# Two gather groups of x instead of six, and one-hot rows made by GpSimd in a graph-network kernel

## The chip, the cores and the metric

The kernel runs on one core of a Trainium2 chip. The metric is device time in microseconds of one execution. A core has a matrix engine (TensorE, PE in the profile; its weight loads are PEld), VectorE (DVE), ScalarE (ACT), GpSimd (POOL) and SyncE (SP), which here only issues transfers. Each engine works through its own queue in order; semaphores tie the queues together. SBUF is the on-chip memory of 128 partitions, PSUM the small memory that TensorE writes to.

## What is computed

x has 6250 nodes of 256 values; 100000 edges (src, dst) come sorted by dst. Cut to what matters:

```python
theta_x = (x[dst] - x[src]) @ theta_w.T + theta_b
phi_x = x[src] @ phi_w.T + phi_b
e = relu(theta_x + phi_x)
out = segment_max(e, dst, num_segments=6250)      # 0 where a node has no edge
y = layernorm(x + out)
```

Since the dst part of an edge is the same for all edges of a node, the kernel needs only b = x @ (phi_w - theta_w).T for every node, the maximum of b[src] over each node's edges, and then relu(maximum + x @ theta_w.T + biases) + x, normalised.

## The kernel before

**Two sets of nodes.** Part 1 is nodes 0 to 1129, part 2 the 5120 nodes after (40 tiles of 128, a tile row being one node). Part 1's edges (some 18,700, 146 steps of 128) are all gathered. For part 2 most edges are not gathered: see "parts" below.

**The front** (lines 704 to 784). The rows b of all nodes are made in 13 shares of up to four tiles: load `x_q`, transpose on PE, copy by ScalarE (`x_t`), multiply with the weights (`ps_b`, line 759), copy out and write to `b_rows` in DRAM. `b_of` does this for a pair of tiles. Beside it, GpSimd gathers the first edges of part 1 straight from x, since `b_rows` isn't there yet: `X_GROUPS` groups of `STEPS` = 8 gathers (one gather is 128 rows of 1 KB, one indirect DMA). Their b is then computed per edge (`x_group`, four pairs by `b_of`), which costs PE work but no wait. Two pauses (short iotas, `paced`) follow each of these gathers.

**Runs.** `run` (line 679) is the running maximum along the steps of a group on VectorE (line 688, one instruction per step of 128 x 256), followed by a write of the group to `maxima_1` or `maxima_2` through SP. The gathered groups live in a ring of six buffers (`RING`), tile name `g`.

**The table and the lists.** VectorE sorts the edges of part 2 into a table (`fill_table`), and per slot of 383 source nodes `choice` picks at most one edge of each destination node (nine calls, two slots each); the rest is packed into lists by `list_pieces`, 232 steps long per partition.

**Parts.** For each of 17 slots and each of 5 chunks of 1024 nodes (85 parts, `slot_part`, line 1056), the chosen b rows are fetched by TensorE: a one-hot matrix `hot` (three blocks of 128 x 1024, the last slot one block) times the slot's rows in `terms`, which are split into two terms of lower precision (`slot_terms`, line 1039). A part is 24 matmuls (line 1075); the result goes into the maximum `acc` by VectorE (line 1086; for slot 0 a copy by ScalarE). One block of `hot` takes VectorE one instruction (line 1065) or ScalarE two (lines 1067 and 1068). Which blocks VectorE makes is `dve_hots`: none until `chunk_heads`, then block 0. The second term is a subtraction on VectorE (line 1054). `want`, the row numbers of a part, comes by a transfer through SP. `hot`, `want` and `terms` have two buffers, `raw` one; a part's first matmul reads block 0.

**GpSimd's order is written out**: `in_turn` (line 506) puts each of its operations behind the one before. With list groups the order is: group of 8 gathers, next group of 8 gathers, and so on. `next_group_1` (line 1385) issues the next group of part 1's gathers, the run of the group before, one `node_place` and n parts. It is called nine times between choices, three times within `list_pieces`, once after; then, as long as groups are left, with two parts each. The three gathers of the list's own rows (`dst_w`) stand between the eleventh and the twelfth of these groups. Then follow the 30 list groups (`gather_2`, from b_rows by `list_src`), with the remaining parts spread among them.

**The end** (lines 1273 to 1374, 1447 to 1453). Shares of up to 8 tiles: gather the list maxima, take the maximum with `acc`, add x @ theta_w.T, relu, add x (`rows_of`), then mean, squares and normalise (`normalise`: squares at line 1328 and the normalising at 1338, both on ScalarE, per tile), and write.

The instructions of one engine are placed by a scheduler at build time, by program order and its own estimate of when inputs are ready; only `in_turn` and `behind_in_order` fix more.

Of the kernel before, what the change touches and what calls it, by code (L numbers as in the profile page):

```python
# [58 lines left out]
X_GROUPS = 6  # L59
# [7 lines left out]
DVE_HOTS = 1  # L67
# [3 lines left out]
X_AFTER = 6  # L71
# [356 lines left out]
def gnn_kernel(ctx: ExitStack, tc: tile.TileContext, x, src, dst, theta_w, theta_b, phi_w, phi_b, out):  # L428
# [71 lines left out]
    paced = [2]  # L500
# [209 lines left out]
    with (  # L710
# [59 lines left out]
        for k, share in enumerate(shares(4)):  # L770
# [266 lines left out]
    dve_hots = [0]  # L1037

    def slot_terms(s):
# [3 lines left out]
        rest = left % P  # L1043
        if whole:
            nc.sync.dma_start(raw[:, :whole, :], flat(b_rows, first * D, [[D, P], [P * D, whole], [1, D]]))
        if left < SLOT_ROWS:
            nc.sync.dma_start(raw[rest : rest + 1, whole, :], maxima_2[0:1, :])
        even = rest // 16 * 16
        for a, b in ((0, even), (even, rest)):
            if b > a:  # L1050
                nc.sync.dma_start(raw[a:b, whole, :], flat(b_rows, (first + whole * P + a) * D, [[D, b - a], [1, D]]))
        terms = terms_of[s] = slots.tile([P, PARTS, KB, D], FR, name="terms")
        nc.scalar.copy(terms[:, 0, :n], raw[:, :n])
        nc.vector.tensor_tensor(terms[:, 1, :n], raw[:, :n], terms[:, 0, :n].bitcast(FP), op=ALU.subtract)

    def slot_part(s, c):
# [54 lines left out]
    def list_chunks(ps):  # L1111
# [4 lines left out]
        chunk_0 = work.tile([P, 1], FP, name="chunk_0")  # L1116
# [21 lines left out]
    def list_places():  # L1138

        has = work.tile([P, TILES], FP, name="has")  # L1140
        nc.vector.tensor_tensor(has, up_to[:, 1:], up_to[:, :TILES], op=ALU.is_gt)
        place_f = work.tile([P, TILES], FP, name="place_f")
        nc.vector.tensor_scalar(place_f, up_to[:, 1:], before, -1.0, op0=ALU.add, op1=ALU.add)
        chunk_of = work.tile([P, TILES], FP, name="chunk_of")
# [5 lines left out]
        step = work.tile([P, TILES], I32, name="step")  # L1150
        group = work.tile([P, TILES], I32, name="group")
# [3 lines left out]
        apart = work.tile([P, TILES], FP, name="apart")  # L1155
# [11 lines left out]
    def list_pieces():  # L1167
# [38 lines left out]
        owner = work.tile([P, 1], I32, name="owner")  # L1206
# [31 lines left out]
    def list_carry():  # L1238

        nodes = wide[:, : BACK + LIST_CHUNK]  # L1240
        same = work.tile([P, BACK], FP, name="same_node")
        n_same = work.tile([P, 3], FP, name="n_same")
# [3 lines left out]
        step = work.tile([P, 1], I32, name="carry_step")  # L1246
        group = work.tile([P, 1], I32, name="carry_group")
# [5 lines left out]
        chunk_1 = work.tile([P, 1], FP, name="chunk_1")  # L1253
# [19 lines left out]
    def rows_of(part, j0, n, ps_tile):  # L1273
# [11 lines left out]
        totals = work.tile([P, STEPS], FP, name="totals", bufs=3)  # L1285
# [35 lines left out]
    def normalise(part, j0, n, x_f, totals):  # L1321

        r = work.tile([P, 5, STEPS], FP, name="r")
# [78 lines left out]
    dve_hots[0] = DVE_HOTS  # L1402
# [7 lines left out]
    paced[0] = 1  # L1410
# [8 lines left out]
    paced[0] = 0  # L1419
# [28 lines left out]
    last_shares = [(2, j, STEPS) for j in range(0, TILES - STEPS, STEPS)]  # L1448
    last_shares += [(2, j, STEPS // 2) for j in (TILES - STEPS, TILES - STEPS // 2)]
# [38 lines left out]
```

## Time and profile before

| | |
|---|---|
| median of 3 runs | 747.21 us (745.25 to 751.66) |
| the profiled execution | 743.81 us, its span 741.9 us |
| PE busy | 650.1 us (88%) |
| DVE busy | 640.0 us (86%) |
| POOL busy | 516.5 us (70%) |
| ACT busy | 493.2 us (66%) |
| part matmuls, line 1075 | 1960, 459.7 us busy |
| list gathers (b_rows by list_src) | 232, mean 1008 ns |
| part 1's gathers from b_rows | 98, mean 1342 ns |
| part 1's gathers from x | 48, mean 1267 ns |
| block 0 of `hot` on DVE, line 1065 | 76, mean 760 ns |
| second terms on DVE, line 1054 | 16 of 768 elements, mean 958 ns |
| first gather from b_rows | 111.9 us |
| gathers of the list's own rows | 260.8 us |
| first list gather | 280.2 us |
| last list gather | 610.3 us |
| first gather of part 2's list maxima | 658.9 us |

Busy time is the time in which an instruction of the engine runs; waits and issue gaps between them do not count. Stretches and starts are in microseconds from the span's start. In lists of instructions, "g<-b_rows,list_src" reads: writes tile g, from b_rows by the numbers in list_src; what stands in brackets is the idle time before it and what ended that.

### The profile page before, as it was taken

What the parts mean: (1) busy time and instruction counts of PE and PEld (TensorE: products, weight loads), DVE (VectorE), ACT (ScalarE), POOL (GpSimd) and SP (SyncE); (2) the same over time, 40 slices, a digit from 0 to 9 for tenths busy, and PEclk for the clock granted to TensorE, in tenths of its full rate; (3) what the DMA queues carried; (4) which work ended last, traced back from release to release, by engine and by line L of the source; (5) the groups of instructions that cost most, each with busy time, mean ns of one, the idle gap of its engine ahead of it and who ended that gap; (6) DMA issues with size and microseconds to landing.
All of it is one profiled execution on the core that took longest, in us unless ns stands there. A gap on an engine that the chain in (4) does not pass through costs nothing.

```text
span 741.9 us, 9973 instructions
## 1 busy us (share of the span) xinstructions
PE 650.1 (88%) x3018; PEld 538.2 (73%) x3018; DVE 640.0 (86%) x1197; ACT 493.2 (66%) x700; POOL 516.5 (70%) x561
## 2 busy tenths in 40 slices
PE   1299999839777899999999999999999999789970
PEld 0288888727565788788888888888888888579970
DVE  6699999999996989598979889798878989968881
ACT  0144444459997678687878778777777877037885
POOL 7788987879887787777777777777746373037720
PEclk9999999959998999999999999999999999999995
DMA  6586745585667777988787888778767686535632
GB/s 208 143 282 209 248 157 194 179 285 161 210 206 258 220 251 232 361 267 255 254 261 227 257 242 266 229 258 277 242 223 213 215 255 212 177 107 187 200 142 116
DMA packets 55893, 164.82 MB, mean 222 GB/s; under 512 B 11835, under 2 KB 19796, under 8 KB 48500
## 3 DMA queue, kind: packets, MB, share of 16 engines
q1 hardware_dynamic: 32344, 98.76, 38.5%
q0 software_dynamic: 20944, 57.62, 27.2%
q10 hardware_dynamic: 2540, 7.69, 2.9%
q8 instruction: 27, 0.44, 0.3%
q14 instruction: 38, 0.31, 0.1%
HBM read 101.08 MB, written 63.74 MB: 222 GB/s over the span
## 4 chain that ended last, share of the span: by engine, by line
PE 46%; DVE 14%; ACT 7%; issue 5%; DMA 4%; POOL 2%; DVEq 0%; ACTq 0%; POOLq 0%; SPq 0%
PE ps_f L1075 44%; ACT x_f L1338 3%; DVE acc L1086 3%; ACT squares L1328 3%; DVE g L688 2%; DMA want<-chosen_rows 2%; POOL g L512 2%; PE ps_e L1299 1%; DVE work L1203 1%; DVE hot L1065 1%; DMA g<-b_rows,src 1%; DVE words L1200 1%; DMA dst_w<-list_words,run_start 1%; ACT x_t L1294 1%; DVE x_f L1314 1%
## 5 line engine op out<-in xcount | busy, mean ns | idle before, releaser
L1075 PE MATMUL ps_f<-hot,terms 128*128 128x512 f32 x1960 | 459.7, 396 | 26.2 <-ACT hot L1068 12.2
L1075 PEld LDWEIGHTS ps_f<-hot,terms 128*128 128x128 f32 x1960 | 372.0, 191 | 109.6 <-ACT hot L1068 15.3
L512 POOL DMA_INDIRECT g<-b_rows,list_src x232 | 233.8, 1008 | 92.6 <-issue 63.3
L1067 ACT ACTIVATE hot<-want,minus_row 128x1024 fp32r<-128x1024 f16 x169 | 186.3, 1147 | 95.1 <-PE ps_f L1075 86.3
L1086 DVE TENSOR_TENSOR acc<-acc,ps_f 128x1024 f32<-128x1024 f32 x160 | 193.5, 1216 | 33.2 <-PE ps_f L1075 32.2
L688 DVE SCALAR_TENSOR_TENSOR g<-g,caps 128x256 f32<-128x256 f32 x376 | 180.6, 480 | 9.7 <-DMA g<-b_rows,src 6.7
L1068 ACT ACTIVATE hot<-hot 128x1024 fp32r<-128x1024 f32 x169 | 169.0, 1046 | 0.0
L512 POOL DMA_INDIRECT g<-b_rows,src x98 | 131.5, 1342 | 29.8 <-issue 25.9
L759 PE MATMUL ps_b<-weights,x_t 128*128 128x256 f32 x388 | 89.5, 385 | 1.3 <-ACT x_t L749 0.5
L512 POOL DMA_INDIRECT g<-maxima,place x49 | 47.7, 973 | 52.2 <-DMA maxima<-g 27.2
L759 PEld LDWEIGHTS ps_b<-weights,x_t 128*128 128x128 f32 x388 | 72.1, 191 | 14.3 <-ACT x_t L749 5.0
L512 POOL DMA_INDIRECT g<-in_x_dram,src x48 | 60.8, 1267 | 11.3 <-issue 7.1
L1065 DVE TENSOR_SCALAR hot<-want,row_id 128x1024 fp32r<-128x1024 f16 x76 | 57.6, 760 | 3.0 <-DMA want<-chosen_rows 2.8
L1299 PE MATMUL ps_e<-weights,x_t 128*128 128x256 f32 x192 | 48.4, 380 | 0.2 <-ACT x_t L1294 0.2
L1299 PEld LDWEIGHTS ps_e<-weights,x_t 128*128 128x128 f32 x192 | 32.8, 190 | 3.6 <-ACT x_t L1294 0.5
L762 ACT COPY g<-ps_b 128x512 f32<-128x512 f32 x24 | 14.1, 586 | 29.8 <-PE ps_b L759 28.7
L762 ACT COPY b_sb<-ps_b 128x512 f32<-128x512 f32 (+1 forms) x25 | 14.5, 578 | 28.8 <-PE ps_b L759 24.8
L1294 ACT COPY x_t<-ps_e 128x512 f32<-128x512 f32 x24 | 13.7, 575 | 29.1 <-PE ps_e L1292 29.1
L1338 ACT ACTIVATE x_f<-x_f,r 128x256 f32<-128x256 f32 x49 | 25.3, 590 | 10.0 <-DVE r L1335 10.0
L488 POOL IOTA pause<- 128x160 f32 x102 | 29.2, 287 | 3.3
L749 ACT COPY x_t<-ps_xt 128x512 f32<-128x512 f32 (+1 forms) x49 | 26.1, 593 | 0.0
L1328 ACT ACTIVATE squares<-x_f,r 128x256 bf16<-128x256 f32 x49 | 24.3, 500 | 1.7 <-DVE r L1325 1.7
(266 smaller groups left out, 503.4 us busy)
## 6 DMA issues: line engine op xcount, KB each, us to landing
maxima<-g SPq DMA_DIRECT2D x47, 1024.0 KB
want<-chosen_rows SPq DMA_DIRECT2D x85, 256.0 KB
x_q<-in_x_dram SPq DMA_DIRECT2D x12, 512.0 KB
b_rows<-b_sb ACTq DMA_DIRECT2D x12, 512.0 KB
x_f<-in_x_dram SPq DMA_DIRECT2D x5, 1024.0 KB
out_dram<-x_f SPq DMA_DIRECT2D x5, 1024.0 KB
raw<-b_rows SPq DMA_DIRECT2D x16, 256.0 KB
g<-b_rows,list_src POOLq DMA_INDIRECT x232, 4.6
```

What stands on the lines that cost most here:

```text
L488: return nc.gpsimd.iota(t, pattern=[[step, t.shape[1]]], base=base, channel_multiplier=per_partition, allow_small_or_imprecise_dtypes=True,)
L512: in_turn(nc.gpsimd.indirect_dma_start(out=out, out_offset=out_offset, in_=in_, in_offset=in_offset))
L688: one = nc.vector.scalar_tensor_tensor(g[:, k, :], last[part], caps[:, t : t + 1], g[:, k, :], op0=ALU.min, op1=ALU.max)
L759: nc.tensor.matmul(ps[:, h, :], x_t[:, h, k, :], weights[:, k, 0, :], start=(k == 0), stop=(k == KC - 1))
L1065: nc.vector.tensor_scalar(hot[:, b, :], want, row_id[:, b : b + 1], None, op0=ALU.is_equal)
L1067: nc.scalar.activation(hot[:, b, :], want, AF.Abs, bias=minus_row[:, b : b + 1], scale=1.0)
L1068: nc.scalar.activation(hot[:, b, :], hot[:, b, :].bitcast(FP), AF.Relu, bias=1.0, scale=-1.0)
L1075: nc.tensor.matmul(ps[:, w : w + 512], terms[:, part, b, h * P : (h + 1) * P], hot[:, b, w : w + 512], start=(i == 0), stop=(i == n - 1),)
L1086: latest_part[0] = nc.vector.tensor_tensor(to, to, ps, op=ALU.max).ins.name
L1299: nc.tensor.matmul(a[:, i, :], x_t[:, 2 * i + c, :], weights[:, c, 1, :], start=(c == 0), stop=False)
L1328: nc.scalar.activation(squares, x_f[:, k, :], AF.Square, bias=mean[:, k : k + 1], scale=1.0, accum_out=var[:, k : k + 1])
L1338: nc.scalar.activation(x_f[:, k, :], x_f[:, k, :], AF.Identity, bias=mean[:, k : k + 1], scale=inv[:, k : k + 1])
```

## The change

X_GROUPS goes from 6 to 2, so that four groups of part 1 more are gathered from `b_rows` and need no product of their own. Since 13 calls of `next_group_1` come before the loop over the groups left, four groups then remain for that loop, with two parts each. Block 0 of `hot` is made by GpSimd instead of VectorE, but only from the list groups on; before that ScalarE makes all blocks. The second terms are made by GpSimd throughout. Both operations stand in GpSimd's written order, so they run between groups of gathers. All pauses behind gathers go. The pools of the part tiles are laid out before the front's, the accumulator behind it. At the end the last tiles are cut into shares of 4, 4, 4, 2 and 2, and for the last 16 tiles VectorE does every second normalisation.

```diff
-X_GROUPS = 6
+X_GROUPS = 2
-DVE_HOTS = 1
+POOL_HOTS = 1
-X_AFTER = 6
...
-    paced = [2]
+    paced = [0]
...
-    acc_pool = body.enter_context(tc.tile_pool(name="accs", bufs=1))
-    acc = acc_pool.tile([P, KC, OWN], FP, name="acc")
-
+    work = body.enter_context(tc.tile_pool(name="work", bufs=2))
+    slots = body.enter_context(tc.tile_pool(name="slots", bufs=2))
...
-            nc.sync.dma_start(present(x_q, *share), node_rows(x, *share))
+            x_loaded = nc.sync.dma_start(present(x_q, *share), node_rows(x, *share)).ins.name
...
-            if k == X_AFTER:
-                x_group(of_x[0])
-        for i in of_x[1:]:
+        for i in of_x:
             x_group(i)
 
-    work = body.enter_context(tc.tile_pool(name="work", bufs=2))
-    slots = body.enter_context(tc.tile_pool(name="slots", bufs=2))
+    acc_pool = body.enter_context(tc.tile_pool(name="accs", bufs=1))
+    acc = acc_pool.tile([P, KC, OWN], FP, name="acc")
...
+        for to, rows in pieces:
+            one = nc.sync.dma_start(to, rows)
+            if s == 0:
+                behind_in_order(one, x_loaded, "x ahead of a slot's rows")
         terms = terms_of[s] = slots.tile([P, PARTS, KB, D], FR, name="terms")
         nc.scalar.copy(terms[:, 0, :n], raw[:, :n])
-        nc.vector.tensor_tensor(terms[:, 1, :n], raw[:, :n], terms[:, 0, :n].bitcast(FP), op=ALU.subtract)
+        in_turn(nc.gpsimd.tensor_tensor(terms[:, 1, :n], raw[:, :n], terms[:, 0, :n].bitcast(FP), op=ALU.subtract))
...
-            if b < dve_hots[0]:
-                nc.vector.tensor_scalar(hot[:, b, :], want, row_id[:, b : b + 1], None, op0=ALU.is_equal)
+            if b < pool_hots[0]:
+                in_turn(nc.gpsimd.tensor_scalar(hot[:, b, :], want, row_id[:, b : b + 1], None, op0=ALU.is_equal))
...
-        totals = work.tile([P, STEPS], FP, name="totals", bufs=3)
+        totals = work.tile([P, STEPS], FP, name="totals", bufs=4)
...
-        r = work.tile([P, 5, STEPS], FP, name="r")
+        shared = part == 2 and j0 >= TILES - 2 * STEPS
+        r = work.tile([P, 5, STEPS], FP, name="r", bufs=4)
...
-            nc.scalar.activation(
-                x_f[:, k, :], x_f[:, k, :], AF.Identity, bias=mean[:, k : k + 1], scale=inv[:, k : k + 1]
-            )
+            if shared and k % 2:
+                nc.vector.tensor_scalar(
+                    x_f[:, k, :], x_f[:, k, :], inv[:, k : k + 1], mean[:, k : k + 1], op0=ALU.mult, op1=ALU.add
+                )
+            else:
+                nc.scalar.activation(
+                    x_f[:, k, :], x_f[:, k, :], AF.Identity, bias=mean[:, k : k + 1], scale=inv[:, k : k + 1]
+                )
...
     chunk_heads()
-    dve_hots[0] = DVE_HOTS
...
     list_carry()
-    paced[0] = 1
...
     n_groups = LIST_GROUPS
-    paced[0] = 0
+    pool_hots[0] = POOL_HOTS
...
-    last_shares = [(2, j, STEPS) for j in range(0, TILES - STEPS, STEPS)]
-    last_shares += [(2, j, STEPS // 2) for j in (TILES - STEPS, TILES - STEPS // 2)]
+    widths = [STEPS] * (TILES // STEPS - 2) + [4, 4, 4, 2, 2]
+    assert sum(widths) == TILES
+    last_shares = [(2, sum(widths[:i]), n) for i, n in enumerate(widths)]
```

The rest of the diff gives some fourteen small tiles of the list stage one buffer instead of two, each of them used once.

More of the change, by code (lines that the diff above doesn't have):

```diff
@@ L768, in x_group @@
             run_1(i)
-        for k, share in enumerate(shares(4)):
+        for share in shares(4):
             n = share[2]
@@ L1043, in slot_terms @@
         rest = left % P
+        pieces = []
         if whole:
-            nc.sync.dma_start(raw[:, :whole, :], flat(b_rows, first * D, [[D, P], [P * D, whole], [1, D]]))
+            pieces.append((raw[:, :whole, :], flat(b_rows, first * D, [[D, P], [P * D, whole], [1, D]])))
         if left < SLOT_ROWS:
-            nc.sync.dma_start(raw[rest : rest + 1, whole, :], maxima_2[0:1, :])
+            pieces.append((raw[rest : rest + 1, whole, :], maxima_2[0:1, :]))
         even = rest // 16 * 16
@@ L1149, in list_places @@
         )
-        step = work.tile([P, TILES], I32, name="step")
-        group = work.tile([P, TILES], I32, name="group")
+        step = work.tile([P, TILES], I32, name="step", bufs=1)
+        group = work.tile([P, TILES], I32, name="group", bufs=1)
         nc.vector.tensor_scalar(
@@ L1245, in list_carry @@
         )
-        step = work.tile([P, 1], I32, name="carry_step")
-        group = work.tile([P, 1], I32, name="carry_group")
+        step = work.tile([P, 1], I32, name="carry_step", bufs=1)
+        group = work.tile([P, 1], I32, name="carry_group", bufs=1)
         nc.vector.tensor_scalar(step, n_same[:, 0:1], -1.0, 0.0, op0=ALU.add, op1=ALU.max)
@@ L1252, in list_carry @@
         )
-        chunk_1 = work.tile([P, 1], FP, name="chunk_1")
+        chunk_1 = work.tile([P, 1], FP, name="chunk_1", bufs=1)
         iota(chunk_1, 0, 1 - STEPS, STEPS)
```

20 lines of the change are left out of this document (10 added, 10 removed).

## Prediction

> **What bounds the kernel now.** I read the busy time by stage first, to see which engine is full where.
>
> ```profile
> 36.00:147.00 111.00, 109.41 (x577) 93.91 (x576) 108.38 (x184) 52.35 (x99) 95.08 (x130) 1.00 0.63 210
> 147.00:245.00 98.00, 67.94 (x256) 50.81 (x256) 89.93 (x175) 81.76 (x130) 82.27 (x58) 0.84 0.70 224
> 280.00:519.00 239.00, 238.05 (x1051) 196.15 (x1050) 208.26 (x323) 185.01 (x185) 181.76 (x180) 1.00 0.82 261
> 611.00:652.00 41.00, 34.15 (x151) 27.12 (x149) 39.86 (x68) 15.56 (x19) 8.22 (x9) 1.00 0.55 183
> 652.00:715.00 63.00, 62.26 (x390) 57.42 (x391) 49.50 (x165) 43.42 (x121) 38.70 (x40) 1.00 0.51 170
> 715.00:742.00 27.00, 4.63 (x28) 4.00 (x26) 9.51 (x44) 18.34 (x55) 0.00 (x0) 0.66 0.30 120
> ```
>
> The columns are the stretch, its length, then PE, weight loads, VectorE (DVE), ScalarE (ACT) and GpSimd (POOL), clock, DMA share, GB/s. From 36 to 147 us PE and DVE are both full (b of all nodes and of six x groups; the edge table). From 147 to 245 PE is a third idle while lists are made. From 245 to 652 PE is full, with the parts. Then come the closing shares (PE full to 715) and an ACT tail. The chain of waits agrees: one piece of it is 310 us of part matmuls.
>
> ```profile
> 313.59 309.53 PE ps_f L1075 x1364
> ```
>
> So PE sets the end of the list stage. How far behind it is GpSimd? Its gathers alone (busy us and count, clock, DMA, GB/s):
>
> ```profile
> 163.50:214.00 50.50, 44.99 (x18) 0.90 0.63 194
> 214.00:260.50 46.50, 35.94 (x35) 0.89 0.76 239
> 279.50:519.00 239.50, 178.35 (x176) 1.00 0.82 260
> 519.00:611.00 92.00, 56.22 (x57) 1.00 0.72 229
> ```
>
> ```profile
> 263.34 0.29 POOL L488 IOTA pause<- 128x160 f32 x1
> ...
> 610.25 0.95 POOL L512 DMA_INDIRECT g<-b_rows,list_src  x1 [0.30 <-issue]
> ...
> 658.93 0.95 POOL L512 DMA_INDIRECT g<-maxima,place  x1 [27.25 <-DMA maxima<-g]
> ```
>
> Until 519 GpSimd never stops: a gather is 1.01 us busy and 0.30 us of issue gap, 1.31 us in all. Only 70% shows as busy, but the engine is full. After 519 its gathers wait for VectorE's runs, which are held by the parts. Without those waits the 57 gathers left would end at 519 + 57 x 1.31 = 594, not 611. The next work, gathers from the finished maxima, could start about 13 us after the last list gather (4.6 median landing, 8 run steps of 0.45, 5.0 for the last maxima write from 653.9 to 658.9); in fact it starts at 658.9. **So GpSimd has 658.9 - 13 - 594 = 52 us of slack**, and that is what the change spends.
>
> **What is removed.** Four of six x groups leave the front: 16 pairs of tiles, each 4 transposes and 8 matmuls. PE does 48.5 pairs from 38 to 147, 2.25 us each, so 36 us leave PE. The part tiles no longer share memory with that stage: the first hot, at 161.6 now, can come when PE is through, near 147 - 36 = 111. By 245 only 224 part matmuls of 1960 were done; PE gains some 35 to 50 us on its own path. From VectorE go 76 hots x 0.76 = 58 us and 17 subtractions, 16 us. If PE stayed the bound, this would be a gain.
>
> **What is added on GpSimd, in its own order.**
>
> (1) Thirty-two gathers of x, which lay in the front beside PE, become gathers of b_rows: 32 x 1.31 = +42 us, after the b_rows writes. That front work was hidden, the new is not.
>
> (2) The b_rows gathers start earlier. They start at 111.9, behind the paced x gathers. The last b_rows write is issued at 101.0 with x group 0 (four pairs, 9 us) ahead of it; without that and with 4.6 us of landing they start at 96.5: -15 us. The ring lets groups 2 to 5 go at once, and group 0's slot is free long before group 6 needs it (about 138).
>
> (3) Fifty-eight hots. By program order 9 + 9 + 1 + 8 = 27 of 85 parts are issued before the list stage, so 58 come after, about two behind each of 29 groups of gathers. No row shows this operation on GpSimd. The nearest are:
>
> ```profile
> L512 POOL DMA_INDIRECT g<-b_rows,list_src x232 | 233.8, 1008 | 92.6 <-issue 63.3 <-DVE g L688 22.7 <-DVE acc L1086 2.3
> ...
> L1054 DVE TENSOR_TENSOR terms<-raw,terms 128x768 fp32r<-128x768 f32 x16 | 15.3, 958 | 6.0 <-ACT terms L1053 6.0
> ...
> L488 POOL IOTA order<- 128x1440 f32 x1 | 1.4, 1352 | 0.0
> ```
>
> The iota writes 1440 elements in 1.35 us, 0.94 ns each, so 1024 that are only written cost 0.96 us: the low end. Twice that, 1.92, for reading and writing by turns is the high end. ScalarE's pass of this shape (L1067) takes 1.15; I take 1.1, near the iota, the only row on this engine. A pause of 0.29 between two gathers lengthens their distance only from 1.25 to 1.40, so 0.15 us of the gap is hidden once per group: 29 x (2 x 1.1 - 0.15) = +59 us (51 to 107).
>
> (4) Seventeen subtractions of 768 elements. Low end 0.72 (the iota's rate), high end 2.17 (two reads and a write by turns); VectorE's row is 0.96. I take 1.3: +22 us (12 to 37). The Trainium skill (GPSIMD Engine Reference, Elementwise — side-by-side cycle accounting) speaks against this edit: an add of two 2048-element inputs takes GpSimd 4497 ns and VectorE 2293. By it an estimate is 1.69 us each, and the total would be 7 us longer than mine; no run here shows it yet.
>
> What stands behind a waiting hot: GpSimd's next eight gathers, then VectorE's run steps, SP's maxima write and the want loads behind that, and on PE the part's first matmul, which reads block 0. I cost such waits at nothing: the hot's buffer is freed by the part two before, and with PE needing 24 x 0.227 = 5.4 us per part against a GpSimd group of about 13 us for two, PE is ahead. If that cover is gone, each part adds its wait to GpSimd, 58 us for 1 us each.
>
> ScalarE makes all blocks of the first 27 parts: 27 x 3 x 2.0 + 10 copies + 9 node places, some 186 us from 107 to 293. The list stage starts at 280 + 42 - 15 = 307, so it is hidden; late by 10 us it would still cost nothing, since PE then has 1312 matmuls x 0.227 = 298 us, to 605, and GpSimd ends far later.
>
> (5) Nothing by themselves: deeper r and totals, single buffers of list tiles (each used once), SP's order of x before slot 0's rows, acc behind the prologue (first written after it anyway), and the lost pauses, which only slowed transfers beside a full PE.
>
> (6) The tail. Eight of the last 16 normalisations go to VectorE (8 x 0.5 = 4 us of ScalarE's backlog after 716), and the last share has 2 tiles, not 4 (two squares and about 1.5 us of normalising less): -7 us, 3 to 10.
>
> **The sum.** Last list gather: 594 + 42 - 15 + 59 + 22 = 702. Then 13 to the first gather of maxima, 83 from there to the end as now (741.9 - 658.9), less 7: span 791. The profiled execution took 743.8 for a span of 741.9, so 793; it lies 3 us under the median of 747.2, and I forecast **794**. With the low ends 685 and 776; with the high ends 765 and 856.
>
> **The rivals.**
>
> *GpSimd's arithmetic hides* (faster). If hots and subtractions run beside descriptor making or in the gap, only the gathers count: last gather 621 + 3, span 624 + 13 + 83 - 7 = 713, time 715; PE ends at 605 and is no bound. It decides if a hot adds under 0.4 us: 621 + 58 x 0.4 + 12 is the 653 at which the end is as now. For it: the pause's 0.15 of 0.29. Against: an iota starts exactly where its gather ends.
>
> *The front's delay is not there* (no change). The 88 gathers before the list's rows took 148.9 us (111.9 to 260.8) where 88 x 1.31 is 115; in 163.5 to 214 a gather took 2.5 us beside VectorE's list steps. If these no longer meet, 34 us go; with the low ends the last gather is at 651 and the time is 742. Against: both stages still overlap.
>
> *VectorE and GpSimd hold each other up* (slower still). If each of the 75 new operations waits out one run step (L688, 0.48 us), 36 us come on top: 830. The slow gathers speak for it; against, in the list stage L688 fills under a third of the time. The Trainium skill (SBUF — State Buffer, SBUF: two separate sides) has VectorE and GpSimd share a port pair that one takes for a whole instruction, an instruction with two SBUF inputs like L688 included; the slow gathers fit, but no run here shows it for arithmetic.
>
> *It does not interleave*: the scheduler places the hots elsewhere and PE waits or not as now; about 747.
>
> **How the numbers follow.** The forecast, GpSimd full to the end of the list, has 0.56; holding each other up 0.14; hiding 0.15; no front delay 0.12, of which a quarter below the bound; not interleaving 0.03. About 1% is what a measurement of this kernel tells from no change. Faster: 0.15 + 0.03 = 0.18. Same: 0.09 + 0.03 = 0.12. Slower: 0.70. The range goes from 735, which takes in the unchanged cases and leaves out hiding, to 840; the forecast's own is 776 to 830.
>
> **What would show it.** GpSimd without waits from 97 to about 700; first list gather near 307 to 315; 58 hots of about 1.1 us; PE idle a fifth of the list stage, waiting for GpSimd's hot; last list gather near 702; about 83 us less 7 after the first maxima gather. A hot of 1 us that lengthens its group by under 0.4, or a first list gather before 280, would prove me wrong.

## The result, and the profile after

| | before | after |
|---|---|---|
| median | 747.03 us (745.25 to 751.66) | 944.97 us (944.47 to 946.71) |
| ratio, with its 95% interval | | 1.264 (1.258 to 1.270) |
| span of the profiled execution | 741.9 us | 944.6 us |
| gathers of the list's own rows | 260.8 us | 279.7 us |
| first list gather | 280.2 us | 347.8 us |
| last list gather | 610.3 us | 830.5 us |
| last part matmul | 650 us | 851 us |

The kernel became slower by a quarter. The direction and the engine were forecast, the size was not: 794 us, with a range that ended at 840.

First the gathers of tile `g` in the kernel after: count, then duration in ns (minimum, median, maximum), first and last start in us.

```profile
L511 POOL DMA_INDIRECT g<-b_rows,list_src x232: 942/952/1193, 347.8 to 830.5; - x116
```

A single gather is as short as before. What grew is the distance from the first list gather to the last: 482.7 us, where it was 330. The first half of that stage by engine (columns as in the prediction: stretch, length, PE, weight loads, VectorE, ScalarE, GpSimd, clock, DMA share, GB/s):

```profile
347.80:600.00 252.20, 189.41 (x713) 149.62 (x712) 148.26 (x173) 134.72 (x136) 203.00 (x153) 0.87 0.52 167
```

GpSimd is busy for 80% of it (85% in the second half), and most of the rest is the 0.30 us behind each gather; PE, which was full here, is down to 75%. The clock granted to PE fell too, from 1.00 in the list stage before to 0.86 over this one, but that is not what makes the stage long: GpSimd's instructions (53 hots 151 us, ten subtractions 18, the gathers and a few small ones 231), 68 us behind the gathers and 15 us in front of two hots add up to all of it. The chain that ended last moved with it, from 46% PE and 2% GpSimd to this:

```profile
POOL 26%; PE 18%; issue 9%; ACT 5%; DVE 4%; DMA 3%; POOLq 0%; SPq 0%; ACTq 0%; DVEq 0%
```

And the two new operations with the run steps (busy us and mean ns; behind the second bar the idle time before them and who ended it):

```profile
L687 DVE SCALAR_TENSOR_TENSOR g<-g,caps 128x256 f32<-128x256 f32 x376 | 234.1, 623 | 29.9 <-DMA g<-b_rows,src 16.3
...
L1066 POOL TENSOR_SCALAR hot<-want,row_id 128x1024 fp32r<-128x1024 f16 x58 | 165.0, 2853 | 17.8 <-ACT hot L1069 12.0
...
L1055 POOL TENSOR_TENSOR terms<-raw,terms 128x768 fp32r<-128x768 f32 (+1 forms) x17 | 30.8, 1812 | 37.8 <-ACT terms L1054 37.7
```

A hot takes 2.85 us, not the 1.1 of the forecast. The other side of that row is PE's: these are its largest two waits (who waited for whom: us in all, times, longest).

```profile
PE ps_f L1076 <- POOL hot L1066: 117.9, 30, 7.2
PE ps_f L1076 <- ACT hot L1069: 47.7, 15, 32.2
```

The second of them, whose longest single wait is 32 us, was in no step of the prediction. Last, GpSimd's order at the end of the list:

```profile
830.46 0.96 POOL L511 DMA_INDIRECT g<-b_rows,list_src  x1 [0.30 <-issue]
831.44 1.00 POOL L1055 TENSOR_TENSOR terms<-raw,terms 128x256 fp32r<-128x256 f32 x1
832.43 5.67 POOL L1066 TENSOR_SCALAR hot<-want,row_id 128x1024 fp32r<-128x1024 f16 x2
...
843.32 5.77 POOL L1066 TENSOR_SCALAR hot<-want,row_id 128x1024 fp32r<-128x1024 f16 x2 [1.21 <-DMA want<-chosen_rows]
849.25 1.05 POOL L511 DMA_INDIRECT g<-maxima,place  x1 [0.15 <-issue]
...
861.16 0.95 POOL L511 DMA_INDIRECT g<-maxima,place  x1 [1.88 <-DVE x_f L1315]
```

The last slot's subtraction and five hots stand between the last list gather and the next one, 17.8 us, and then the eight gathers of part 1's share, which ran at 621 us before, inside a wait. The 40 gathers of part 2 start at 861.2.

Some of the experiments ran on chips where the kernel before itself took 914 to 923 us; what makes those chips slower is not known. Their times are set beside those of runs on the same chip, unless the text says otherwise.

### The profile page after: what moved, and what is told of

It is laid out like the page before. It is cut to its first block, busy times and chain, and to the rows that moved or that the text cites. A ratio compares the mean times of both kernels' runs of the same rounds, so it can differ in the third digit from the quotient of the medians.

```text
span 944.6 us, 9523 instructions
## 1 busy us (share of the span) xinstructions
PE 683.9 (72%) x2826; PEld 547.4 (58%) x2826; DVE 644.0 (68%) x1130; ACT 506.5 (54%) x698; POOL 645.8 (68%) x540
## 4 chain that ended last, share of the span: by engine, by line
POOL 26%; PE 18%; issue 9%; ACT 5%; DVE 4%; DMA 3%; POOLq 0%; SPq 0%; ACTq 0%; DVEq 0%
PE ps_f L1076 15%; POOL g L511 15%; POOL hot L1066 10%; DMA want<-chosen_rows 3%; ACT x_f L1345 2%; ACT squares L1330 2%; PE ps_e L1300 2%; DVE g L687 2%; ACT hot L1068 1%; DMA g<-b_rows,src 1%; ACT x_t L1295 1%; POOL terms L1055 1%; DVE g L1311 0%; PE ps_e L1293 0%; DVE x_f L1315 0%
## 5 line engine op out<-in xcount | busy, mean ns | idle before, releaser
L1076 PE MATMUL ps_f<-hot,terms 128*128 128x512 f32 x1960 | 524.8, 431 | 192.0 <-POOL hot L1066 117.9
L1076 PEld LDWEIGHTS ps_f<-hot,terms 128*128 128x128 f32 x1960 | 408.5, 211 | 305.2 <-POOL hot L1066 130.8
L1068 ACT ACTIVATE hot<-want,minus_row 128x1024 fp32r<-128x1024 f16 x187 | 205.7, 1144 | 285.0 <-PE ps_f L1076 172.3
L687 DVE SCALAR_TENSOR_TENSOR g<-g,caps 128x256 f32<-128x256 f32 x376 | 234.1, 623 | 29.9 <-DMA g<-b_rows,src 16.3
L1066 POOL TENSOR_SCALAR hot<-want,row_id 128x1024 fp32r<-128x1024 f16 x58 | 165.0, 2853 | 17.8 <-ACT hot L1069 12.0
L757 PE MATMUL ps_b<-weights,x_t 128*128 128x256 f32 x260 | 62.7, 396 | 9.1 <-ACT x_t L747 8.7
L757 PEld LDWEIGHTS ps_b<-weights,x_t 128*128 128x128 f32 x260 | 50.1, 198 | 18.1 <-ACT x_t L747 11.5
L1055 POOL TENSOR_TENSOR terms<-raw,terms 128x768 fp32r<-128x768 f32 (+1 forms) x17 | 30.8, 1812 | 37.8 <-ACT terms L1054 37.7
L511 POOL DMA_INDIRECT g<-in_x_dram,src x16 | 18.9, 1181 | 9.8 <-issue 7.1
L1303 PE MATMUL ps_e<-bias_terms,pick 128*128 128x256 f32 x48 | 23.0, 480 | 0.0
```

Source lines behind the costliest of these rows:

```text
L511: in_turn(nc.gpsimd.indirect_dma_start(out=out, out_offset=out_offset, in_=in_, in_offset=in_offset))
L687: one = nc.vector.scalar_tensor_tensor(g[:, k, :], last[part], caps[:, t : t + 1], g[:, k, :], op0=ALU.min, op1=ALU.max)
L757: nc.tensor.matmul(ps[:, h, :], x_t[:, h, k, :], weights[:, k, 0, :], start=(k == 0), stop=(k == KC - 1))
L1055: in_turn(nc.gpsimd.tensor_tensor(terms[:, 1, :n], raw[:, :n], terms[:, 0, :n].bitcast(FP), op=ALU.subtract))
L1066: in_turn(nc.gpsimd.tensor_scalar(hot[:, b, :], want, row_id[:, b : b + 1], None, op0=ALU.is_equal))
L1068: nc.scalar.activation(hot[:, b, :], want, AF.Abs, bias=minus_row[:, b : b + 1], scale=1.0)
```

## The experiments

### Which part of the change costs what

Four kernels split the change. Three start from the kernel after and put arithmetic back on VectorE:

```diff
-                in_turn(nc.gpsimd.tensor_scalar(hot[:, b, :], want, row_id[:, b : b + 1], None, op0=ALU.is_equal))
+                nc.vector.tensor_scalar(hot[:, b, :], want, row_id[:, b : b + 1], None, op0=ALU.is_equal)
```

(hots alone),

```diff
-        in_turn(nc.gpsimd.tensor_tensor(terms[:, 1, :n], raw[:, :n], terms[:, 0, :n].bitcast(FP), op=ALU.subtract))
+        nc.vector.tensor_tensor(terms[:, 1, :n], raw[:, :n], terms[:, 0, :n].bitcast(FP), op=ALU.subtract)
```

(subtractions alone), and both. The fourth starts from the kernel before and makes block 0 on GpSimd from the list groups on:

```diff
...
-            if b < dve_hots[0]:
+            if b < pool_hots[0]:
+                in_turn(nc.gpsimd.tensor_scalar(hot[:, b, :], want, row_id[:, b : b + 1], None, op0=ALU.is_equal))
+            elif b < dve_hots[0]:
...
     n_groups = LIST_GROUPS
     paced[0] = 0
+    pool_hots[0] = 1
```

What was expected of them, hots on VectorE first, then both, then subtractions on VectorE, then the fourth:

> The changed kernel with block 0 of hot made by VectorE from the list groups on; the second terms stay on GpSimd. Theory Q (what counts is GpSimd's own queue: 58 hots of 2.85 us in series with the gathers): the list stage still starts near 348 us; 232 gathers at 1.27 and 11 subtractions of 1.86 end it near 348 + 295 + 20 = 663, then some 95 us to the end: 755 to 770 us. Theory P (the port: the hots' main harm is that they stretch VectorE's run steps from 0.48 to 0.70 and hold parts up): VectorE's steps go back to 0.48, but GpSimd's queue had room for the hots, so the gain is under 80 us: above 860. Theory F (the loss is made in the front, before the first list gather): still above 880.

> The changed kernel with neither block 0 of hot nor the second terms on GpSimd (both on VectorE, block 0 only from the list groups on). Left of the change: two x groups, the pools' places, no pauses, the tail. Theory W (a subtraction on GpSimd is a wait across three queues: SP's load of the next slot's rows waits for it, the want loads wait behind that load, ScalarE and PE behind those): the first list gather moves from 348 to 295 to 305 and ScalarE's two long waits for want (30 and 24 us) go; the end near 700 to 725 us. Theory A (the front is bound by ScalarE, which makes all blocks of 27 parts): the first list gather stays past 325 and the time is 735 to 760.

> The changed kernel with only the second terms moved back to VectorE; 58 hots stay on GpSimd. Theory Q: list stage 295 + 165 us of GpSimd's queue; by theory W the first list gather comes some 45 us earlier and 20 us of subtractions leave the list stage: 875 to 890 us. By theory A only the 20 us go: 920 to 930.

> The kernel before, with the one edit that from the list groups on block 0 of hot is made by GpSimd, in its order (76 hots were VectorE's, about 66 of them move). Theory Q: the gathers unhindered would end at 594; 66 x 2.85 - 15 = 173 us on top, then 96 to the end: about 863 us. Theory P: the gathers' queue absorbs the 52 us of slack and more, time under 800. If six x groups instead of two make the hots harmless: 747.

Measured, the first four on one chip where the kernel before took 748.8 us; the last row is the kernel after from the table above, where before took 747.0:

| | median us | ratio to before | first list gather | last list gather |
|---|---|---|---|---|
| hots on VectorE | 812.0 | 1.083 (1.072 to 1.093) | 345.1 | 684.4 |
| both on VectorE | 757.7 | 1.010 (1.003 to 1.018) | 334.4 | 644.1 |
| subtractions on VectorE | 902.8 | 1.204 (1.191 to 1.216) | 331.2 | 791.1 |
| before + hots on GpSimd | 897.9 | 1.197 (1.185 to 1.209) | 279.1 | 784.9 |
| after | 945.0 | 1.264 | 347.8 | 830.5 |

The hots alone cost 902.8 - 757.7 = 145 us, or 945.0 - 812.0 = 133 with the subtractions there. In the kernel before 66 hots move; by GpSimd's time less its slack that is 66 x 2.85 - 52 = 136 us, and 149 were measured. The subtractions cost 54 without hots and 42 with them, more than their 17 x 1.81 = 31 us of GpSimd time. Not all of the forecasts were met: by GpSimd's queue alone the hots on VectorE should have given 755 to 770 us (812.0 measured) and the fourth kernel 863 (897.9), and the subtractions on VectorE fell between the two readings. What makes up these 35 to 57 us was not tested. All the rest together (groups of x, pauses, block 0 on ScalarE ahead of the list, memory order, tail) is worth 9 to 11 us, and that small sum hides larger numbers: the list starts 54 us later than before, first to last list gather is 20 us shorter (309.7 for 330.1), and so is what comes after it (112.1 for 131.6).

### The price of a hot by itself

Why 2.85 us? In the kernel before, behind its last share in program order, GpSimd ran each of eight forms three times (`row_id` and the constants are operands; the half-precision input is `half`; the tiles are made above the lines shown):

```diff
...
+    for _ in range(3):
+        nc.gpsimd.tensor_scalar(rounded[:, 0, :], half, row_id[:, 0:1], None, op0=ALU.is_equal)
+        nc.gpsimd.tensor_scalar(single[:, 0, :], half, row_id[:, 0:1], None, op0=ALU.is_equal)
+        nc.gpsimd.tensor_scalar(single[:, 0, :], single[:, 1, :], row_id[:, 0:1], None, op0=ALU.is_equal)
+        nc.gpsimd.tensor_scalar(single[:, 0, :512], single[:, 1, :512], row_id[:, 0:1], None, op0=ALU.is_equal)
+        nc.gpsimd.tensor_scalar(single[:, 0, :], single[:, 1, :], row_id[:, 0:1], None, op0=ALU.add)
+        nc.gpsimd.tensor_scalar(single[:, 0, :], single[:, 1, :], 2.0, None, op0=ALU.add)
+        nc.gpsimd.tensor_copy(single[:, 0, :], single[:, 1, :])
+        nc.gpsimd.tensor_tensor(single[:, 0, :], single[:, 1, :], single[:, 0, :], op=ALU.subtract)
```

> The kernel before with 24 GpSimd operations of 128 x 1024 (one of 512) added behind its last share, where VectorE is idle; each form three times: the hot as it is (f16 in, fp32r out, is_equal with a per-partition operand), the same to f32, the same f32 to f32, that with 512 elements, add with a per-partition operand, add of a constant, a plain copy, and the two-input subtraction. Theory O (2.85 us is the operation's own price): the hot costs 2.8 to 2.9 us here too, and the forms tell what in it is dear. Theory P (2.85 is a price beside VectorE's work, by the shared port): it falls to 1.0 to 1.5 us. If only the format is dear, the f32 forms cost about 1.0 and the f16 ones 2.85; if it is the per-partition operand, the constant add is cheap and all others dear. The time of the whole: before plus some 45 us.

The groups of that run (mean ns behind the comma; L1469 to L1476 are the eight forms in the order above):

```profile
L1470 POOL TENSOR_SCALAR single<-half,row_id 128x1024 f32<-128x1024 f16 x3 | 8.6, 2855 | 0.2
L1473 POOL TENSOR_SCALAR single<-single,row_id 128x1024 f32<-128x1024 f32 x3 | 8.6, 2852 | 0.3
L1469 POOL TENSOR_SCALAR rounded<-half,row_id 128x1024 fp32r<-128x1024 f16 x3 | 8.5, 2842 | 65.0 <-DVE r L423 65.0
L1471 POOL TENSOR_SCALAR single<-single,row_id 128x1024 f32<-128x1024 f32 x3 | 8.5, 2839 | 1.1 <-DMA g<-maxima,place 1.0
...
L1474 POOL TENSOR_SCALAR single<-single 128x1024 f32<-128x1024 f32 x3 | 8.3, 2769 | 0.3
...
L1476 POOL TENSOR_TENSOR single<-single 128x1024 f32<-128x1024 f32 x3 | 7.0, 2338 | 0.3
...
L1472 POOL TENSOR_SCALAR single<-single,row_id 128x512 f32<-128x512 f32 x3 | 4.7, 1558 | 0.2
...
L1475 POOL COPY single<-single 128x1024 f32<-128x1024 f32 x3 | 3.1, 1037 | 0.2
```

Neither the input's type nor the output's, nor the comparison, nor the operand from memory is what is dear: an addition of a constant takes 2.77 us. It is the form, tensor with scalar, which costs (2839 - 1558) / 512 = 2.5 ns an element and, as an estimate from these two sizes, 1558 - 512 x 2.5 = 278 ns besides. A copy of the same tile takes 1.04 us. The hot's price is GpSimd's own and needs no collision with VectorE, which did nothing beside the later repeats. (The three of the hot's exact form, L1469, ran while the last share was ending; the later repeats of L1470, L1471 and L1473 cost the same.)

### A hot at the price that was forecast

The copy makes it possible to run the prediction's own sum: the same instruction stream, with 1.04 us where the comparison stood. From the list on this kernel leaves out the comparison of block 0, so its results are not those of the program; only its time is read.

```diff
-                in_turn(nc.gpsimd.tensor_scalar(hot[:, b, :], want, row_id[:, b : b + 1], None, op0=ALU.is_equal))
+                in_turn(nc.gpsimd.tensor_copy(hot[:, b, :], want))
```

> The changed kernel, with GpSimd's 58 hots made by a copy of want instead of the comparison: the comparison of block 0 is left out from the list on, all waits and the order stay. Measured by itself, a copy of 1024 elements took GpSimd 1.04 us, the comparison 2.85. Theory G (GpSimd's own time sets the list stage, and only the hot's price was mis-sized): the time falls by 58 x 1.8 = 105 us, to 0.888 of the changed kernel, 1.12 of before; hots of 1.04 to 1.2 us. Rival W (the waits around a hot on another engine cost as much as its time): it falls by less than 60 us, 1.18 of before or more.

It took 925.6 us beside 913.6 for the kernel before. With no run of the kernel after on that chip this decides nothing, so both were run side by side:

> The changed kernel once more, as the measure for the next three on whatever chip they run: 1.264 of before where before takes 747 us; nearer to before on a chip where before takes 914, since there other work waits longer.

> The copy in the comparison's place again (block 0's comparison left out from the list on), now beside the changed kernel on one chip. Theory G (GpSimd's own time): 58 x 1.8 = 105 us less than the changed kernel. Rival W (the waits): less than 60 us less.

The kernel after took 1027.6 us there (1.116 of before, 1.105 to 1.127), the copy 928.7 (1.014, 1.003 to 1.024): 99 us less, where GpSimd's own time says 105 and the rival said less than 60. The gathers of tile `g` and the hots, in the kernel after,

```profile
L511 POOL DMA_INDIRECT g<-b_rows,list_src x232: 942/953/1204, 387.9 to 871.5; - x116
...
L1066 POOL TENSOR_SCALAR hot<-want,row_id x58: 2831/2851/2881, 410.1 to 887.0; 128x1024 fp32r<-128x1024 f16 x58
```

and with the copy:

```profile
L511 POOL DMA_INDIRECT g<-b_rows,list_src x232: 943/949/1228, 380.1 to 773.5; - x116
...
L1066 POOL CAST hot<-want x58: 1032/1047/1133, 401.8 to 786.9; 128x1024 fp32r<-128x1024 f16 x58
```

The list stage is 483.6 us in the one and 393.4 in the other. The 90 us between them are nearly all of the difference. Two more things can be read here. The stage of the kernel after is as long on this chip as on the first (483.6 and 482.7), although the whole kernel takes 83 us more: what GpSimd's own instructions set is the same, and the 83 us lie ahead of it (40) and behind it (43). And 393.4 is close to what the prediction's working gives with a hot of 1.1 us, 702 - 307 = 395. That they agree to 2 us is partly luck: the working has all 58 hots, all 17 subtractions and no wait in this stage, while the run has 53 and 10, gathers that are shorter than 1.31 us, and 23 us in front of hots.

### The subtraction: its time or its waits

In the kernel after, the subtraction of a slot stands in GpSimd's order between gathers. `raw` has one buffer, so SP may load the next slot's rows only when the subtraction has read the last ones, and SP's queue holds the `want` loads behind that. SP's own waits for the subtraction, before and after (us in all, times, longest):

```profile
SPq L1045 <- DVE terms L1054: 13.5, 5, 3.5
...
SPq L1050 <- POOL terms L1055: 231.0, 15, 39.3
```

The timeline of the kernel after shows the longest of PE's waits (start, us, engine; SPq is a transfer's issue):

```profile
164.41 1.81 POOL L1055 TENSOR_TENSOR terms<-raw,terms 128x768 fp32r<-128x768 f32 x1
...
166.25 1.36 SPq L1050 DMA_DIRECT2D raw<-b_rows  x3
...
174.52 1.15 ACT L1068 ACTIVATE hot<-want,minus_row 128x1024 fp32r<-128x1024 f16 x1 [29.85 <-DMA want<-chosen_rows]
...
178.49 3.78 PE L1076 MATMUL ps_f<-hot,terms 128*128 128x512 f32 x8 [32.17 <-ACT hot L1069]
```

The subtraction ends at 166.2, SP's loads go out at once, and ScalarE has waited 29.9 us for its `want`, PE 32.2 for the hot. So this is the 32 us wait of the list above. Is it the line, or still the 1.81 us? The kernel with hots on VectorE was run with GpSimd's share of the subtraction cut to 8 of 256 columns; GpSimd's waits stay, and VectorE makes the other columns.

```diff
-        in_turn(nc.gpsimd.tensor_tensor(terms[:, 1, :n], raw[:, :n], terms[:, 0, :n].bitcast(FP), op=ALU.subtract))
+        nc.vector.tensor_tensor(terms[:, 1, :n, 8:], raw[:, :n, 8:], terms[:, 0, :n, 8:].bitcast(FP), op=ALU.subtract)
+        in_turn(nc.gpsimd.tensor_tensor(terms[:, 1, :n, :8], raw[:, :n, :8], terms[:, 0, :n, :8].bitcast(FP), op=ALU.subtract))
```

> The changed kernel with the hots on VectorE from the list on (1.08 of before when run so), and with the subtraction split: VectorE takes columns 8 to 255, GpSimd columns 0 to 7, so GpSimd's share of it falls from 1.86 us to some 0.3 and every wait of the changed kernel stays. Theory W (a slot's copy, subtraction, rows and want stand in line across three queues, and that line costs, not GpSimd's time): at least two thirds of the 54 us stay, 1.06 to 1.09 of before. Rival P (it is GpSimd's time, 17 x 1.86 = 32 us, and what hangs on it): it falls to 1.02 to 1.04.

> The changed kernel with the hots on VectorE from the list on again, as the measure for the next: 1.08 of before where before takes 747 us.

> The last kernel with GpSimd's share of the subtraction cut to 8 of 256 columns (0.38 us instead of 1.86), beside it on one chip. Theory W (the line across three queues costs): within 15 us of it. Rival P (GpSimd's time and what hangs on it): 17 x 1.5 = 25 us or more less.

The first run gave 1.099 of before (1.074 to 1.124), again without its partner. Side by side: 1008.7 us with the whole subtraction, 1013.8 with 3% of it. GpSimd's subtraction fell to a median of 0.25 us and nothing was won. GpSimd waited 166 us before it with the whole subtraction, and as the waits of the narrow one have it:

```profile
POOL terms L1056 <- ACT terms L1054: 203.9, 12, 29.9
```

That fits the line and not the time, with two limits. VectorE has 15 us of subtractions in the second kernel that it has not in the first, which could hide a gain. And on that chip GpSimd is not what bounds these two kernels: it is busy for 46 and 47% of the span, and the list stage takes 457.1 us with the whole subtraction, where the same kernel took 339.3 on the first chip. In the kernel after GpSimd is full in the list stage, and there the time counts: the stage is 22.8 us longer than with the subtractions on VectorE (482.7 for 459.9), and ten subtractions take 18.3 of them. Another 16.6 us lie ahead of the list (347.8 for 331.2), where GpSimd waited 39.1 us for VectorE when it had no subtractions, which points at the line there.

The kernel before with the subtractions alone moved also pays more than the time:

> The kernel before with only the second terms' subtraction on GpSimd, in its order. Theory Q (queue time): 17 x 1.86 = 32 us lie within the 52 us of slack, no change, 740 to 752. Theory W (three queues wait on it: SP's load of the next slot's rows, the want loads behind that, ScalarE, PE): 20 to 50 us more, 765 to 800, with ScalarE's waits for want well over the 10 us of before.

It took 983.8 us beside 914.2 (1.082, 1.076 to 1.089): 70 us for 33 us of work, with 172 us in which GpSimd stood before a subtraction. A second buffer for `raw` would cut the line at SP; it wasn't tried.

### The late start of the list

With no arithmetic on GpSimd, and four groups of x fewer, the list still starts at 334.4 us. The waits of that kernel:

```profile
DVE g L687 <- DMA g<-b_rows,src: 39.4, 21, 4.8
...
POOL dst_w L511 <- DVE place_f L1162: 34.7, 1, 34.7
```

GpSimd waits 34.7 us for VectorE before the gathers of the list's rows, and VectorE has waited 39.4 us in its run steps for gathers (6.7 before). Two kernels were to tell what makes it late. Six groups of x with all else as in the kernel with both on VectorE:

```diff
-X_GROUPS = 2
+X_GROUPS = 6
```

> The changed kernel without arithmetic on GpSimd and with six x groups again: what is left of the change is the pools' places, no pauses, block 0 on VectorE only from the list groups on, and the tail. Theory G (two x groups are what makes the list late: 32 more gathers, and parts' accumulation on VectorE ahead of the list's instructions): the first list gather moves from 334 back to 280 to 295, with 19 parts issued ahead of it instead of 27; the end 735 to 750 us. Rival (the list is late because the pools moved and parts start early, whatever the groups): first list gather above 315 and no gain over 757.

> The changed kernel without arithmetic on GpSimd and with six groups of x again, as run once on a chip where before took 914 us (0.997 of before there). If the late list of the two-group version (first list gather 334 us for 280) comes from the groups of x, this one starts its list within 8 us of before's 280 on a chip where before takes 747, and then is faster than before by 2 to 5%, since its list stage was 41 us shorter with two groups; rival: with fewer parts done ahead of the list the stage is as long as before's 370, and it is within 1% of before.

and two groups with no parts issued ahead of the list:

```diff
         choice(s0)
         wanted(s0)
-        next_group_1(1)
+        next_group_1(0)
...
         if i in (3, 7, 14):
-            next_group_1(1)
-        else:
-            fetch_parts(i % 2)
-    next_group_1(1)
+            next_group_1(0)
+    next_group_1(0)
```

> The changed kernel without any arithmetic on GpSimd (1.01 of before; first list gather at 334.4 us), and without the 27 parts that the 13 calls before the list issue: all parts come with the last groups of part 1 and the list. Theory V (VectorE sets the start of the list: some 18 more maxima of parts than before, 1.22 us each, stand ahead of its list steps): first list gather 22 us or more earlier, 300 to 313. Rival R (VectorE's run steps, waiting for the later gathers, hold its list steps up): first list gather within 8 us of 334. The end is later in both if PE then has too much left: 1.02 to 1.08 of before.

With six groups the kernel took 0.997 of before (0.992 to 1.002) and, a second time, 1.004 (0.993 to 1.016), and the list started at 299.5 and 299.3 us. On the slower chips the kernels with two groups and subtractions on GpSimd started it at 372 to 409 us (on the first chip the subtractions were worth 11 to 17 of that, 345.1 for 334.4 and 347.8 for 331.2), and those with before's groups and pauses at 304 to 327. This points at the groups of x and speaks against the lost pauses, but no two kernels that differ in the groups alone were run on one chip, so it is not shown. The gain of 2 to 5% that one reading expected of six groups, on a chip where before takes 747 us, did not come on one where it takes 923: the list started at 299.3 us, but the list stage took 436.5. That the shorter stage with two groups comes from the parts done ahead of a late list is likely, but was not tested alone. Without early parts the list started at 349.4 us (963.2 us beside 913.6). The kernel that it should be set against wasn't run on that chip, so whether VectorE is held up by its maxima of parts or by waiting for gathers stays open.

### The tail alone

The kernel before with shares of 4, 4, 4, 2 and 2 tiles, VectorE's half of the normalising, and the buffers that these need:

```diff
-    last_shares = [(2, j, STEPS) for j in range(0, TILES - STEPS, STEPS)]
-    last_shares += [(2, j, STEPS // 2) for j in (TILES - STEPS, TILES - STEPS // 2)]
+    widths = [STEPS] * (TILES // STEPS - 2) + [4, 4, 4, 2, 2]
+    assert sum(widths) == TILES
+    last_shares = [(2, sum(widths[:i]), n) for i, n in enumerate(widths)]
```

> The kernel before with the tail of the changed one alone: last shares of 4, 4, 4, 2 and 2 tiles, every second normalisation of the last 16 tiles on VectorE, r and totals with four buffers (six list tiles with one buffer instead of two, to make room). My step (6): 7 us less, 3 to 10. Rival: nothing or up to 3 us more, since in the changed kernel and its variants the stretch from the last part matmul to the end was 92 to 94 us, against 92 before.

> The kernel before with the edit of the last shares alone, as run once already on a chip with a lower clock (0.98 of before there). By the prediction's step 6 it saves 3 to 10 us, 0.987 to 0.996 of before. A rival: nothing, since 91 to 94 us lay between the last part's matmul and the end in all kernels.

> The kernel before with the edit of the last shares alone, a third time, beside the last one. By the prediction's step 6 it saves 3 to 10 us, 0.987 to 0.996 of before; rival: nothing, 0.997 to 1.003.

Three runs gave 0.980 (0.974 to 0.987), 1.005 (0.999 to 1.011) and 926.4 us beside 922.8. They contradict each other, so no saving is shown. The profiles on the first chip show none either: from the first gather of part 2's maxima behind the last wait to the end it is 944.6 - 861.2 = 83.4 us in the kernel after, 756.2 - 672.2 = 84.0 with both on VectorE, and 741.9 - 658.9 = 83.0 before.

No version that was run is faster than the kernel before by more than can be measured, the tail's first run excepted.

## Why the prediction was right in direction and wrong in size

The prediction's sum and the profile after, in the same four stretches:

| | forecast | measured | missing |
|---|---|---|---|
| to the first list gather | 307 | 347.8 | 41 |
| first to last list gather | 395 | 482.7 | 88 |
| to the gathers of part 2's maxima | 13 | 30.7 | 18 |
| from there to the end | 76 | 83.4 | 7 |
| span | 791 | 944.6 | 154 |

**The bound: right.** GpSimd is the engine that ends the list stage, and the slack of 52 us fits the kernel before with hots alone to 13 us (136 for 149). The rivals in which the arithmetic hides, or the scheduler puts it elsewhere, are out: a hot added 2.3 to 2.5 us (133 and 145 over 58, 149 over 66). So is the rival without the front's delay: the list started later than forecast. The range left out the sum's own high end, 856, without a reason; but no end of it held a hot of 2.85 us.

**Step 3, the hots: the failing step.** The price was bounded by 0.96 and 1.92 us, from an iota that only writes and from twice that for reading and writing by turns, and 1.1 was taken. It is 2.85, outside both ends. A rate per element written was carried from one form of instruction to another; the run of single prices shows that it holds for a copy (1.04) and not for tensor with scalar. Of the 58 hots, 53 lie in the list stage and take 151 us for the 59 forecast: 92 us more. Waits in front of two hots add 15, gathers shorter than forecast and seven fewer subtractions take some 19 off, which leaves the 88 us missing there. The other five hots come behind the last list gather, where the step had spread all of them among the groups: with the last subtraction and two short waits they are 17.8 us of the 30.7 at the end of the list. The rest, the last list gather itself, eight gathers of part 1's share and a wait of 1.9 us, comes to the 13 of the forecast by luck, since these gathers were not in it.

**Step 4, the subtractions: price low, cover wrong.** 1.81 us on average for 1.3, which is 9 us in all. The Trainium skill (GPSIMD Engine Reference, Elementwise — side-by-side cycle accounting) gave an estimate of 1.69, nearer than mine; two inputs of 1024 elements took 2.34 us by themselves, and half of the page's 4497 ns, an estimate, would be 2.25. The larger error is the sentence that such waits cost nothing. The prediction named what stands behind a waiting operation, SP's `want` loads among it, but only for the hots, and it took PE to be ahead. The subtraction waits for ScalarE's copy, and SP's next loads wait for the subtraction; 42 to 54 us went there for 22 forecast.

**Steps 1 and 2, the gathers: the work right, the early start lost.** From the list's rows to the first list gather the kernel with both on VectorE takes 334.4 - 273.7 = 60.7 us, and the forecast was 19.4 + 42. GpSimd also starts at 94.6 for the forecast 96.5. But the 15 us were to carry through to the list, and they meet VectorE: the gathers of the list's rows start 13 us later than before there (19 in the kernel after) instead of 15 earlier. That is 24 to 27 of the 41 us missing ahead of the list (331.2 and 334.4 with the subtractions on VectorE, for 307); the subtractions add the rest. The step treated the front as GpSimd's alone, though the first windows that it quotes show VectorE full in it.

**Steps 5 and 6.** The small edits and the tail together cost nothing that the runs could tell (0.997 and 1.004 with six groups, each to about 1%). The tail's 7 us are not seen: ScalarE is busy for 11.5 us of the last 27.6, where it was 18.3 of the last 26.9, and the stretch is as long as before.

**The rival that the engines hold each other up** was right in what it describes and wrong in what it costs. Run steps went from a mean of 482 ns with no arithmetic on GpSimd to 579 with the hots alone and 623 in the kernel after, 376 x 0.14 = 53 us more of VectorE. But VectorE waits 212 us for PE in that kernel, a hot takes 2853 ns in it where it takes 2842 by itself, and in the list stage GpSimd waits 0.5 us for run steps. So GpSimd, which sets the end, loses next to nothing.

## What to carry to other kernels

A price taken from another form of instruction on the same engine is no bound: here a copy, a subtraction of two tensors and a comparison with a scalar of the same size cost 1.04, 2.34 and 2.85 us. Before work is moved to an engine with known slack, that one price is worth a run by itself, in the very form that will be used. And an operation that is put in the written order of a queue ties three queues together: ask not only what its own time is, but who must have finished before it and which loads wait for the buffer that it reads.

## What the runs showed of the hardware

GpSimd's tensor with scalar costs about 0.28 us plus 2.5 ns an element, an estimate from 512 and 1024 elements. With half and single precision in and two formats out, comparing or adding, 1024 elements took 2.77 to 2.86 us, more than the 2.34 of tensor with tensor. The Trainium skill (GPSIMD Engine Reference, Engine selection) calls one-input work on GpSimd "roughly line-rate". The copy, with 1.04 us for 1024 elements, is near that; the comparison takes 2.85 against VectorE's 0.76, and here the measurement decides.

VectorE's run steps, which read two operands from SBUF, stretch where a hot of GpSimd starts, and its maxima of parts, which read one from PSUM, do not. From the timeline of the kernel after (two hots on GpSimd, a maximum, four run steps, and of these the first and the last two by themselves):

```profile
554.83 5.68 POOL L1066 TENSOR_SCALAR hot<-want,row_id 128x1024 fp32r<-128x1024 f16 x2
555.89 1.22 DVE L1087 TENSOR_TENSOR acc<-acc,ps_f 128x1024 f32<-128x1024 f32 x1 [1.50 <-PE ps_f L1076]
557.03 3.60 DVE L687 SCALAR_TENSOR_TENSOR g<-g,caps 128x256 f32<-128x256 f32 x4
...
557.03 2.04 DVE L687 SCALAR_TENSOR_TENSOR g<-g,caps 128x256 f32<-128x256 f32 x1
...
559.63 1.00 DVE L687 SCALAR_TENSOR_TENSOR g<-g,caps 128x256 f32<-128x256 f32 x2
```

The maximum takes its usual 1.22 us. The first run step, during which the second hot starts (557.67), takes 2.04 us; the three after it take about 0.5 each, though that hot runs until 560.5. The whole trace has the same picture: 27 of the 376 run steps have a hot starting within them, and these take 2.18 us on average, and each of them ends 1.38 to 1.42 us after the hot's start; of the 62 that begin while a hot runs and see none start, 59 take less than 0.6. The hots are no longer for it (2.85 us with and without such a step). The Trainium skill (SBUF — State Buffer, SBUF: two separate sides) has the port pair that the two engines share held for a whole instruction, while the other engine blocks fully. A run step that is held up beside a hot agrees with that; steps of 0.5 us within a hot of 2.85 do not, and here the measurement decides.
